# Assembling sixteen rows of x ahead of time, and fetching one channel from SBUF

## The chip, the cores and the metric

The kernel runs on one core of a Trainium2 chip. The metric is the device time of one execution in microseconds (us); the median of three runs of the kernel before the change is 3288.08 us (3287.99 to 3289.75). Lower is better. A core has five engines that follow their own instruction streams in order: TensorE (PE in the profile; its weight loads are PEld), VectorE (DVE), ScalarE (ACT), GpSimd (POOL) and SyncE (SP, which here only starts transfers). Transfers are moved by 16 DMA engines; the kernel starts them from SP, a few from ACT, and those that add to their destination from POOL. All data are 32-bit floats.

## The reference, cut to what matters

The input x is a 384 x 384 grid of vectors of 128 channels. Two layers follow each other.

Layer 0 normalises each vector over its channels to z, forms `left` and `right`, each a matrix product of z times a sigmoid gate of z, and multiplies them channel by channel:

```python
core = jnp.einsum('bikh,bjkh->bijh', left, right)
zo = _layernorm(core, onorm_g, onorm_b) @ Wout + bout
g = jax.nn.sigmoid(x @ Wg + bg)
return x + g * zo
```

So for each of 128 channels `core` is a 384 x 384 x 384 matrix product, and the following layer norm goes over the channels: its statistics are complete only when the last channel is.

Layer 1 works on each row of the result: `left * right_sum * gate`, where `right_sum` is a sum over the row, then a product with `W_out`, the residual, and a layer norm over the channels.

## The kernel before, in words

There are three stages. The order on each engine is the order of the program's text, since every instruction goes through `seq`, which keeps it.

**Stage 1** (0 to about 1131 us of the profile) walks over x in chunks, normalises, transposes (line 279), makes `left` and `right` (lines 331 to 342) and writes them channel by channel to DRAM as `lr_d`. On the way it stores two other things in DRAM: the transposed rows of `x - nd`, where `nd` is one number per vector made from its mean and deviation, as `xt_d` (line 302), and these numbers as `nd_d` (line 310). Thus x, transposed, is `nd_d` broadcast to all partitions plus `xt_d`.

**Stage 2** (about 1131 to 1875 us) is a loop over the 128 channels h. For each h there are nine matmuls of 128x384 (line 501), each of which the profile shows as two instructions, with `t` (left) and `rr` (right) as operands. `load_h` (lines 86 to 95) loads channel h+3 when h is done with its buffer; `fill(h + 1)` on POOL copies the right part out of the interleaved load (lines 476 to 483); ACT copies the product out of PSUM (line 510) and squares it (511), DVE adds both to the running sums `csum` and `csq` (512, 513), and SP stores the channel to `core_d` (517). The last channel, h = 127, is handled apart (lines 518 to 536): block 0 of its product, rows 0 to 127 of the output, is computed first and stored in two parts (first 16 rows, then 112), then DVE finishes the variance of those rows, ACT takes the square root, and DVE's `inverse` and `newton` give the reciprocal standard deviation `r` (lines 427 to 449). POOL then sends `r` to DRAM as `rstd_d` (line 533) and squares and adds the other two blocks (lines 534 to 536).

**Stage 3** (about 1875 us to the end) is a software pipeline over the 384 rows. Iteration t contains, in this order: `front`, which transposes rows of x if needed and makes the layer-0 gate; the loads that are due; `scale_core(t)`, core times `r` (`cs`); `layer0(t - 2)`, the output product `pr` of layer 0 (line 674) and two DVE instructions that give `x1T`; `gated_left(t - 3)`, two matmuls of layer 1 (691, 692); and for rows whose group's sum is known, `layer1`, the statistics and the norms. Rows 0 to 3 take `r` not from DRAM but through a matmul with a column of the identity (`pb`, line 662), and their `cs` is made by DVE (663); from row 4 on POOL makes it (665) with `rt`, read from `rstd_d`. No `cs` can be made before all 128 channels of the row's `ct` have arrived.

For rows below TR = 16, x comes from the input itself: four rows at a time are loaded (line 570), each row is transposed by three PE instructions (line 640) and copied out of PSUM by ACT or DVE (642, 644). From row 16 on, `load_x` broadcasts `nd_d` into SBUF (576) and `add_x` lets POOL start a transfer that adds `xt_d` to it (584); no transpose is needed. `front` runs ahead of the rows: A = 9 rows at t = 0, and at least L = 4 rows for x, with the gate L rows behind.

At the start of stage 3 SP's order is: x of rows 0 to 11 (three loads), core of rows 0 to 3 in two parts (channels 0 to 111, then 112 to 127), x of rows 12 to 15, then core and `rt` of rows 4 to 7.

Of the kernel before, what the change touches and what calls it, by code (L numbers as in the profile page):

```python
# [8 lines left out]
F32 = mybir.dt.float32  # L9
AF = mybir.ActivationFunctionType  # L10
ALU = mybir.AluOpType
# [3 lines left out]
P = 128  # L15
# [4 lines left out]
def triangle_then_gated_row_kernel(ctx: ExitStack, tc: tile.TileContext, a: dict, out: bass.AP):  # L20
# [9 lines left out]

    nc = tc.nc
    x = a["x"].rearrange("b i j c -> (b i) j c")
    y = out.rearrange("b i j c -> (b i) j c")
    N, _, C = x.shape
# [6 lines left out]
    KEEP = 2  # L43
    RG = 4
    A = 9
    L = 4
    TR = 16

    cpool = ctx.enter_context(tc.tile_pool(name="const", bufs=1))
# [3 lines left out]
    rstd_d = dpool.tile([N, N], F32, name="rstd_d")  # L53
    xt_d = dpool.tile([C, N, NB, P], F32, name="xt_d")
    nd_d = dpool.tile([N, N], F32, name="nd_d")

    def seq(ins):

        return tc.keep_in_program_order(ins)
# [21 lines left out]
    with ExitStack() as ctx2:  # L81
# [369 lines left out]
        with tc.tile_pool(name="p2r", bufs=2, side="right", reuse_waits="tile") as rrp, \  # L451
# [14 lines left out]
            def fill(h):  # L466

                if h < H:
# [15 lines left out]
                    if h == 0:  # L484
                        stay()

            fill(0)
            for h in range(H):
                fill(h + 1)
                t, rr = loaded2.pop(h), right.pop(h)  # L490
                pc = ps.tile([P, NB, 512], F32, tag="pc", name="pc")
                banks = [pc[:, ib, :N] for ib in range(NB)]
                order = [(kb, ib) for kb in range(NB) for ib in range(NB)]
                if h == H - 1:


                    banks[0] = ps1.tile([P, 512], F32, name="pc0")[:, :N]
                    order.sort(key=lambda o: o[1] > 0)
                    seq(nc.scalar.activation(warm, mhalf[:, 0:1], AF.Sqrt, scale=-1.0))
                for kb, ib in order:  # L500
                    seq(nc.tensor.matmul(  # L501
                        banks[ib], lhsT=t[:, kb, ib * P:(ib + 1) * P, 0], rhs=rr[:, kb],
                        start=(kb == 0), stop=(kb == NB - 1),
                    ))

                ct = op.tile([P, NB, N], F32, tag="ct", name="ct")
                sq = qp.tile([P, NB, N], F32, tag="sq", name="sq")
                to = core_d[:, h, :].rearrange("(b p) j -> p b j", p=P)
                if h < H - 1:
                    seq(nc.scalar.copy(ct, pc[:, :, :N]))  # L510
                    seq(nc.scalar.activation(sq, ct, AF.Square))
                    seq(nc.vector.tensor_add(csum, csum, ct))  # L512
                    seq(nc.vector.tensor_add(csq, csq, sq))
                    load_h(h + 3)

                    queue = nc.sync if h < H - 3 else nc.scalar
                    seq(queue.dma_start(out=to, in_=ct))
                else:
                    seq(nc.scalar.copy(ct[:, 0], banks[0]))
                    seq(nc.scalar.activation(sq[:, 0], ct[:, 0], AF.Square))  # L520
                    seq(nc.scalar.dma_start(out=to[:16, 0], in_=ct[:16, 0]))
                    seq(nc.scalar.dma_start(out=to[16:, 0], in_=ct[16:, 0]))
                    seq(nc.vector.tensor_add(csum[:, 0], csum[:, 0], ct[:, 0]))
                    seq(nc.vector.tensor_add(csq[:, 0], csq[:, 0], sq[:, 0]))
                    seq(nc.scalar.copy(ct[:, 1:], pc[:, 1:, :N]))
                    variance(0, slice(0, N))
                    root(0)
                    inverse(0, slice(0, N))
                    newton(0, slice(0, N))
                    seq(nc.scalar.dma_start(out=to[:, 1:], in_=ct[:, 1:]))  # L530


                    seq(nc.gpsimd.dma_start(out=rstd_d[0:P, :], in_=roots[0][1]))
                    seq(nc.gpsimd.tensor_tensor(sq[:, 1:], ct[:, 1:], ct[:, 1:], ALU.mult))
                    seq(nc.gpsimd.tensor_tensor(csum[:, 1:], csum[:, 1:], ct[:, 1:], ALU.add))
                    seq(nc.gpsimd.tensor_tensor(csq[:, 1:], csq[:, 1:], sq[:, 1:], ALU.add))
# [5 lines left out]
    with ExitStack() as ctx3:  # L542
        def pool(name, bufs, **kw):
            return ctx3.enter_context(tc.tile_pool(name=name, bufs=bufs, reuse_waits="tile", **kw))


        xp, lp, fp, inp = pool("p3x", 6), pool("p3l", 20), pool("p3f", A), pool("p3in", 3)
        wp, sp, op, up = pool("p3w", 4), pool("p3s", 4), pool("p3out", 3), pool("p3u", 18)
        ps2, ps = pool("p3ps2", 4, space=PSUM), pool("p3ps", 4, space=PSUM)

        def bank(name):
            return ps.tile([P, 512], F32, tag="bank", name=name)

        def work(name, pool=wp):
            return pool.tile([P, N], F32, tag=name, name=name)

        def work_x(name):

            return lp.tile([P, N], F32, tag="x", name=name)

        cols = [slice(b * P, (b + 1) * P) for b in range(NB)]
        lnsb = lns.unsqueeze(1).to_broadcast([P, NB, C])
# [2 lines left out]

        def load_x(i0):

            if i0 < TR:
                xt = xin[i0] = xp.tile([P, RG, N], F32, tag="xt", name="xn")
                seq(nc.sync.dma_start(  # L570
                    out=xt.rearrange("p i (b c) -> p i b c", b=NB),
                    in_=x[i0:i0 + RG].rearrange("i (b p) c -> p i b c", p=P),
                ))
            elif i0 < N:
                xt = xts[i0] = xp.tile([P, RG, N], F32, tag="xt", name="xt")
                seq(nc.sync.dma_start(
                    out=xt.rearrange("p i j -> p (i j)"),
                    in_=nd_d[i0:i0 + RG].rearrange("i j -> (i j)").partition_broadcast(P),
                ))

        def add_x(i0):
# [4 lines left out]
                    in_=xt_d[:, i0:i0 + RG].rearrange("c i b k -> c (i b k)"), accum_op=ALU.add,  # L586
                ))

        def load_core(i0):
            if i0 < N:  # L590
                ct = inp.tile([P, RG, N], F32, tag="ct", name="ct")

                for hs in (slice(0, H),) if i0 > 0 else (slice(0, H - 16), slice(H - 16, H)):
                    seq(nc.sync.dma_start(out=ct[hs], in_=core_d[i0:i0 + RG, hs].rearrange("i h j -> h i j")))
                rt = None
                if i0 > 0:
                    rt = inp.tile([P, RG, N], F32, tag="rt", name="rt")
                    seq(nc.sync.dma_start(
                        out=rt.rearrange("p i j -> p (i j)"),
                        in_=rstd_d[i0:i0 + RG].rearrange("i j -> (i j)").partition_broadcast(P),  # L600
                    ))
                cin[i0] = ct, rt
# [20 lines left out]

        def front(f):

            r = rows.get(f - L)
            if r:
                pg = bank("pg")
                seq(nc.tensor.matmul(pg[:, :N], lhsT=wg0, rhs=r["xT"], start=True, stop=True))  # L629
                gT = r["gT"] = work("gT", fp)  # L630
                seq(nc.scalar.activation(gT, pg[:, :N], AF.Sigmoid, bias=bg0))  # L631
            if f < N:
                i0, n = f // RG * RG, f % RG
                if f >= TR:
                    xT = xts[i0][:, n]
                else:
                    xT = work_x("xT")
                    pxt = ps2.tile([P, 512], F32, tag="py", name="pxt") if f < A else bank("pxt")
                    for s in cols:
                        seq(nc.tensor.transpose(pxt[:, s], xin[i0][:, n, s], ident))  # L640
                    if 4 <= f < A:
                        seq(nc.vector.tensor_copy(xT, pxt[:, :N]))
                    else:
                        seq(nc.scalar.copy(xT, pxt[:, :N]))
                rows[f] = {"xT": xT}

        def right_sums(i0, i1):

# [18 lines left out]
        def layer0(i):  # L667

            r = rows[i]
            m, n = group[i]  # L670
            if n == 0:
                quad[m] = {"tot": sp.tile([P, 16], F32, tag="tot", name="tot")}
            pr = bank("pr")
            seq(nc.tensor.matmul(pr[:, :N], lhsT=wc, rhs=r["cs"], start=True, stop=True))  # L674
            seq(nc.vector.scalar_tensor_tensor(pr[:, :N], pr[:, :N], bz, r["gT"], ALU.add, ALU.mult))
            x1T = r["x1T"] = work_x("x1T")
            seq(nc.vector.scalar_tensor_tensor(
                x1T, pr[:, :N], bout1, r["xT"], ALU.add, ALU.add, accum_out=quad[m]["tot"][:, n:n + 1]
            ))
# [104 lines left out]
                ))  # L784
            stores.clear()

        for i0 in range(0, 3 * RG, RG):
            load_x(i0)
        load_core(0)
        load_x(3 * RG)  # L790
        load_core(RG)

        pieces = [(variance, b, s) for b in range(1, NB) for s in cols]
        pieces += [(root, b, None) for b in range(1, NB)]
# [1 line left out]
        f, fetched, added = 0, TR, TR  # L796
        for t in range(N + 3):

            while f < min(N + L, t + max(L, A - t // 3)):
                front(f)  # L800
                f += 1
            if t % RG == 0:
                load_core(t + 2 * RG)
            if t >= 2 and fetched <= f + 16:
                load_x(fetched)
                fetched += RG
            if t >= 9 and t % 4 == 1:
# [88 lines left out]
```

## Time and profile before

| | |
|---|---|
| median of three runs | 3288.08 us |
| the profiled execution's own time | 3288.67 us |
| its span, first to last instruction | 3286.9 us |
| PE busy | 3266.7 us, 99% of the span |
| DVE, ACT, POOL busy | 2489.0, 1933.7, 2280.3 us |
| PE transposes of x in stage 3 (line 640) | 48 instructions |
| bytes moved | 873.71 MB, 266 GB/s over the span |

"Busy" is the time in which an engine had an instruction in work; on PE instructions overlap, so that the duration of one is longer than the step from one to the next. A line such as L501 is that line of the kernel. "Idle before, releaser" says what ended an engine's wait. The span lies 1.8 us below the profiled execution's own time, and that time is 0.6 us above the median.

### The profile page before, as it was taken

The page shows a single profiled execution, that of the slowest core. Times are in us where ns is not written, and L with a number is a line of the kernel's source. Part 1 is how long each engine was busy: PE and PEld are TensorE (multiplying, and loading weights), DVE is VectorE, ACT ScalarE, POOL GpSimd, SP SyncE. Part 2 cuts the span into 40 slices and gives each one's busy share as a digit, 9 for nine tenths or more (in the row PEclk, how much of TensorE's full clock was granted, in tenths as well). Part 3 has the DMA queues.
Part 4 walks back from the last instruction along what each step waited for, and adds up shares of the span by engine and source line. Part 5 has one row for each costly group of instructions (what it writes and reads, how often), then busy time and mean ns, then how long its engine had stood idle before and what let it go on. Part 6 is the DMA issues. An engine that isn't in the chain of part 4 may idle for free.

```text
span 3286.9 us, 48330 instructions
## 1 busy us (share of the span) xinstructions
PE 3266.7 (99%) x12460; PEld 1989.3 (61%) x12460; DVE 2489.0 (76%) x8022; ACT 1933.7 (59%) x4056; POOL 2280.3 (69%) x3301
## 2 busy tenths in 40 slices
PE   9999999999999999999999999999999999999998
PEld 4544444444444566666666666667777777777776
DVE  7777777777777655555555688888888888888888
ACT  4555555555555533333333467677777777777776
POOL 6555555555555555556666578888888888888997
PEclk9999999999999999999999999999999999999999
DMA  6998998999999499999999999999999999999994
GB/s 164 274 278 259 276 282 259 276 280 265 271 279 271 147 280 282 285 284 282 282 282 283 285 294 266 279 276 272 273 280 277 269 278 276 272 272 274 268 253 128
DMA packets 922055, 873.71 MB, mean 266 GB/s; under 512 B 24834, under 2 KB 836868, under 8 KB 921780
## 3 DMA queue, kind: packets, MB, share of 16 engines
q1 hardware_dynamic: 906532, 796.03, 78.5%
q0 software_dynamic: 13440, 72.56, 12.8%
q8 instruction: 102, 1.67, 0.2%
q10 hardware_dynamic: 1808, 2.03, 0.2%
q14 instruction: 173, 1.42, 0.1%
HBM read 508.63 MB, written 361.89 MB: 265 GB/s over the span
## 4 chain that ended last, share of the span: by engine, by line
PE 92%; POOL 5%; ACT 1%; issue 1%; DVE 1%; DMA 0%; POOLq 0%; ACTq 0%; DVEq 0%
PE pr L331 30%; PE pc L501 22%; PE py L703 7%; PE pg L629 6%; PE pl L692 6%; PE pr L674 6%; PE pg L691 6%; PE pt L279 4%; PE py L704 3%; POOL rs L723 1%; POOL yt L773 1%; POOL cs L665 1%; ACT py L738 1%; POOL nm L726 0%; POOL rs L722 0%
## 5 line engine op out<-in xcount | busy, mean ns | idle before, releaser
L331 PE MATMUL pr<-wz,zt 128*128 128x512 f32 x2304 | 1039.9, 593 | 0.0
L340 ACT ACTIVATE sg<-pr,rs 128x256 f32<-128x256 f32 x1152 | 482.9, 470 | 497.7 <-PE pr L331 363.8
L501 PE MATMUL pc<-rr,lrh 128*128 128x384 f32 x2304 | 743.3, 486 | 0.3 <-DVE lr L342 0.3
L342 DVE SCALAR_TENSOR_TENSOR lr<-pr,rs,sg 128x256 f32<-128x256 f32 x1152 | 504.6, 480 | 267.4 <-ACT sg L340 219.0
L331 PEld LDWEIGHTS pr<-wz,zt 128*128 128x128 f32 x2304 | 414.6, 191 | 410.7 <-issue 345.2
L501 PEld LDWEIGHTS pc<-rr,lrh 128*128 128x128 f32 x2304 | 452.4, 196 | 291.4 <-issue 1.1
L738 ACT ACTIVATE py<-py,nm,rs 128x128 f32<-128x128 f32 x1149 | 493.0, 430 | 197.8 <-POOL rs L727 116.8
L703 PEld LDWEIGHTS py<-wo,u 128*128 128x128 f32 x2304 | 376.8, 191 | 97.4
L512 DVE TENSOR_TENSOR csum<-csum,ct 128x1152 f32<-128x1152 f32 x127 | 179.1, 1410 | 337.9 <-ACT ct L510 337.9
L665 POOL TENSOR_TENSOR cs<-ct,rt 128x384 f32<-128x384 f32 x380 | 426.0, 1125 | 10.7 <-DMA rt<-rstd_d 5.4
L773 POOL TENSOR_TENSOR yt<-yt,lnb 128x384 f32<-128x384 f32 x380 | 423.8, 1117 | 3.1 <-DVE yt L767 3.1
L510 ACT COPY ct<-pc 128x1152 f32<-128x1152 f32 x127 | 142.1, 1119 | 445.3 <-PE pc L501 441.6
L703 PE MATMUL py<-wo,u 128*128 128x128 f32 x2304 | 402.1, 275 | 0.0
L260 POOL TENSOR_SCALAR sd<-mv 128x8 f32<-128x8 f32 (+1 forms) x145 | 28.5, 197 | 427.4 <-DVE mv L247 427.3
L270 POOL TENSOR_TENSOR z<-xt,nd 128x512 f32<-128x512 f32 x287 | 298.7, 1041 | 36.1 <-POOL z L270 30.9
L718 DVE BATCH_NORM_STATS2 st<-py 128x6 f32<-128x128 f32 x1152 | 265.6, 286 | 68.5 <-PE py L704 66.5
L704 PE MATMUL py<-ident,x1T 128*128 128x128 f32 x1152 | 314.1, 273 | 0.0
L674 PE MATMUL pr<-cs,wc 128*128 128x384 f32 x768 | 313.9, 491 | 0.0
L692 PE MATMUL pl<-x1T,mat_L_conv_W_left 128*128 128x384 f32 x768 | 311.0, 487 | 0.9 <-ACT gT L631 0.8
L691 PE MATMUL pg<-x1T,mat_L_conv_W_gate 128*128 128x384 f32 x768 | 310.8, 487 | 1.0 <-ACT g L694 0.9
L629 PE MATMUL pg<-xt,mat_L_conv_Wg 128*128 128x384 f32 x736 | 298.9, 488 | 1.3 <-ACT gT L631 1.3
L482 POOL COPY rr<-lrh 128x768 f32<-128x768 f32 x128 | 182.7, 1427 | 160.7 <-DMA lrh<-lr_d 160.2
(134 smaller groups left out, 4898.1 us busy)
## 6 DMA issues: line engine op xcount, KB each, us to landing
lr_d<-lr SPq DMA_DIRECT2D x128, 1024.0 KB, 7.2
lrh<-lr_d SPq DMA_DIRECT2D x128, 768.0 KB, 7.8
xt_d<-zt SPq DMA_DIRECT2D x288, 256.0 KB, 5.4
xt<-in_x_dram SPq DMA_DIRECT2D x143, 512.0 KB, 6.5
ct<-core_d SPq DMA_DIRECT2D x95, 768.0 KB, 6.2
rt<-rstd_d SPq DMA_DIRECT2D x95, 768.0 KB, 7.7
out_dram<-yt SPq DMA_DIRECT2D x94, 768.0 KB, 8.8
core_d<-ct SPq DMA_DIRECT2D x125, 576.0 KB, 8.8
```

The source lines that it names most:

```text
L331: seq(nc.tensor.matmul(pr[:, r, :], lhsT=zts[n, q][:, 2 * half + r, :], rhs=wz, start=True, stop=True))
L340: seq(nc.scalar.activation(sg[r], pr[:, r, 2 * H:], AF.Sigmoid, scale=rs[r]))
L342: seq(nc.vector.scalar_tensor_tensor(t[:, :, c * XR + r0 + r, :], pr[:, r, :2 * H].rearrange("k (h s) -> k h s", s=2), rs[r], sg[r].rearra ...
L501: seq(nc.tensor.matmul(banks[ib], lhsT=t[:, kb, ib * P:(ib + 1) * P, 0], rhs=rr[:, kb], start=(kb == 0), stop=(kb == NB - 1),))
L629: seq(nc.tensor.matmul(pg[:, :N], lhsT=wg0, rhs=r["xT"], start=True, stop=True))
L665: seq(nc.gpsimd.tensor_tensor(cs, ct[:, i % RG], rt[:, i % RG], ALU.mult))
L674: seq(nc.tensor.matmul(pr[:, :N], lhsT=wc, rhs=r["cs"], start=True, stop=True))
L691: seq(nc.tensor.matmul(pg2[:, :N], lhsT=wgate, rhs=r["x1T"], start=True, stop=True))
L692: seq(nc.tensor.matmul(pl[:, :N], lhsT=wleft, rhs=r["x1T"], start=True, stop=True))
L703: seq(nc.tensor.matmul(py[:, s], lhsT=r["u"][:, s], rhs=r["wo"], start=True, stop=False))
L738: seq(nc.scalar.activation(py[:, s], py[:, s], AF.Identity, bias=bias, scale=scale))
L773: seq(engine.tensor_tensor(yt, yt, lnbb, ALU.add))
```

## The change

Four things are changed.

1. In stage 2, `early_x(h)` puts together the transposed x of rows 0 to 15, one row in every five channels: SP broadcasts a row of `nd_d` into a buffer (h = 6 + 5i), POOL starts a transfer that adds `xt_d` (h = 8 + 5i), and SP stores the result to a new DRAM tensor `xf_d` (h = 11 + 5i).
2. Stage 3 loads the first 16 rows from `xf_d`, four rows at a time, already transposed. The transposes, their copies out of PSUM and the distance L are gone; `front` is the gate alone, one row ahead at least and nine at t = 0. Nine gates use eight PSUM buffers of both pools.
3. Block 0 of the last channel is copied to a tile of its own, `last_h`, and stored to `core_d` in one transfer. For rows 0 to 3 the last channel no longer comes through `core_d`: four transfers on POOL's queue copy one row each from `last_h` into partition 127 of `ct`. SP's second part now holds channels 111 to 126 (16 partitions).
4. SP's order at the start of stage 3 becomes: x of rows 0 to 7, core channels 0 to 111, x of rows 8 to 11, core channels 111 to 126, core and `rt` of rows 4 to 7, x of rows 12 to 15. Loads of later rows of x are called by the row in work (t + 18) and no longer by the row of `front`. Buffers: `x1T` 18 of its own, `gT` 12 (were 9), `u` 17 (were 18).

```diff
+            def early_x(h):
+                for n, step in enumerate((6, 8, 11)):
+                    i, odd = divmod(h - step, 5)
+                    if not odd and 0 <= i < TR:
+                        if n == 0:
+                            early[i] = rp.tile([P, N], F32, tag="ve", name="xe", bufs=NB)
+                            seq(nc.sync.dma_start(out=early[i], in_=nd_d[i].partition_broadcast(P)))
+                        elif n == 1:
+                            seq(nc.gpsimd.dma_start(
+                                out=early[i], in_=xt_d[:, i].rearrange("c b k -> c (b k)"), accum_op=ALU.add
+                            ))
+                        else:
+                            seq(nc.sync.dma_start(out=xf_d[:, i], in_=early.pop(i)))
...
+            last_h = rp.tile([P, N], F32, tag="r", name="last_h", bufs=NB)
             fill(0)
             for h in range(H):
                 fill(h + 1)
+                early_x(h)
...
-                    seq(nc.scalar.copy(ct[:, 0], banks[0]))
-                    seq(nc.scalar.activation(sq[:, 0], ct[:, 0], AF.Square))
-                    seq(nc.scalar.dma_start(out=to[:16, 0], in_=ct[:16, 0]))
-                    seq(nc.scalar.dma_start(out=to[16:, 0], in_=ct[16:, 0]))
+                    seq(nc.scalar.copy(last_h, banks[0]))
+                    seq(nc.scalar.activation(sq[:, 0], last_h, AF.Square))
+                    seq(nc.scalar.dma_start(out=to[:, 0], in_=last_h))
...
-        xp, lp, fp, inp = pool("p3x", 6), pool("p3l", 20), pool("p3f", A), pool("p3in", 3)
-        wp, sp, op, up = pool("p3w", 4), pool("p3s", 4), pool("p3out", 3), pool("p3u", 18)
+        xp, lp, fp, inp = pool("p3x", 6), pool("p3l", 18), pool("p3f", A + 3), pool("p3in", 3)
+        wp, sp, op, up = pool("p3w", 4), pool("p3s", 4), pool("p3out", 3), pool("p3u", 17)
...
-                for hs in (slice(0, H),) if i0 > 0 else (slice(0, H - 16), slice(H - 16, H)):
+                for hs in (slice(0, H),) if i0 > 0 else (slice(0, H - 16), slice(H - 17, H - 1)):
                     seq(nc.sync.dma_start(out=ct[hs], in_=core_d[i0:i0 + RG, hs].rearrange("i h j -> h i j")))
+                    if i0 == 0 and hs.start == 0:
+                        for i in range(RG):
+                            seq(nc.gpsimd.dma_start(out=ct[H - 1:H, i], in_=last_h[i:i + 1]))
+                    if between and hs.start == 0:
+                        between()
...
-            r = rows.get(f - L)
-            if r:
-                pg = bank("pg")
-                seq(nc.tensor.matmul(pg[:, :N], lhsT=wg0, rhs=r["xT"], start=True, stop=True))
-                gT = r["gT"] = work("gT", fp)
-                seq(nc.scalar.activation(gT, pg[:, :N], AF.Sigmoid, bias=bg0))
-            if f < N:
-                i0, n = f // RG * RG, f % RG
-                if f >= TR:
-                    xT = xts[i0][:, n]
-                else:
-                    xT = work_x("xT")
-                    pxt = ps2.tile([P, 512], F32, tag="py", name="pxt") if f < A else bank("pxt")
-                    for s in cols:
-                        seq(nc.tensor.transpose(pxt[:, s], xin[i0][:, n, s], ident))
-                    if 4 <= f < A:
-                        seq(nc.vector.tensor_copy(xT, pxt[:, :N]))
-                    else:
-                        seq(nc.scalar.copy(xT, pxt[:, :N]))
-                rows[f] = {"xT": xT}
+            r = rows[f] = {"xT": xts[f // RG * RG][:, f % RG]}
+            pg = ps2.tile([P, 512], F32, tag="py", name="pg") if f < A and f % 2 == 0 else bank("pg")
+            seq(nc.tensor.matmul(pg[:, :N], lhsT=wg0, rhs=r["xT"], start=True, stop=True))
+            gT = r["gT"] = work("gT", fp)
+            seq(nc.scalar.activation(gT, pg[:, :N], AF.Sigmoid, bias=bg0))
...
-        for i0 in range(0, 3 * RG, RG):
-            load_x(i0)
-        load_core(0)
+        load_x(0)
+        load_x(RG)
+        load_core(0, between=lambda: load_x(2 * RG))
+        load_core(RG)
         load_x(3 * RG)
-        load_core(RG)
...
-            while f < min(N + L, t + max(L, A - t // 3)):
+            while f < min(N, t + max(1, A - t // 2)):
                 front(f)
                 f += 1
             if t % RG == 0:
                 load_core(t + 2 * RG)
-            if t >= 2 and fetched <= f + 16:
+            if t >= 2 and fetched <= t + 18:
```

In the program's order on POOL the four transfers of `last_h` stand behind line 533 (`rstd_d`) and lines 534 to 536, since stage 3's text comes after stage 2's; in `front` nine gates stand ahead of the first `pb`, a tenth behind it, then two more `pb`, and then `pr` of row 0.

More of the change, by code (lines that the diff above doesn't have):

```diff
@@ L45, in triangle_then_gated_row_kernel @@
     A = 9
-    L = 4
     TR = 16
@@ L55, in triangle_then_gated_row_kernel @@
     nd_d = dpool.tile([N, N], F32, name="nd_d")
+    xf_d = dpool.tile([C, TR, N], F32, name="xf_d")
     def seq(ins):
@@ L485, in fill @@
                         stay()
+            def early_x(h):
[11 more added lines that the diff above has]
+                            seq(nc.sync.dma_start(out=xf_d[:, i], in_=early.pop(i)))
+            early = {}
+            last_h = rp.tile([P, N], F32, tag="r", name="last_h", bufs=NB)
             fill(0)
@@ L518, in triangle_then_gated_row_kernel @@
                 else:
-                    seq(nc.scalar.copy(ct[:, 0], banks[0]))
-                    seq(nc.scalar.activation(sq[:, 0], ct[:, 0], AF.Square))
-                    seq(nc.scalar.dma_start(out=to[:16, 0], in_=ct[:16, 0]))
-                    seq(nc.scalar.dma_start(out=to[16:, 0], in_=ct[16:, 0]))
-                    seq(nc.vector.tensor_add(csum[:, 0], csum[:, 0], ct[:, 0]))
+                    seq(nc.scalar.copy(last_h, banks[0]))
+                    seq(nc.scalar.activation(sq[:, 0], last_h, AF.Square))
+                    seq(nc.scalar.dma_start(out=to[:, 0], in_=last_h))
+                    seq(nc.vector.tensor_add(csum[:, 0], csum[:, 0], last_h))
                     seq(nc.vector.tensor_add(csq[:, 0], csq[:, 0], sq[:, 0]))
@@ L555, in work @@
             return pool.tile([P, N], F32, tag=name, name=name)
-        def work_x(name):
-            return lp.tile([P, N], F32, tag="x", name=name)
         cols = [slice(b * P, (b + 1) * P) for b in range(NB)]
@@ L566, in load_x @@
         def load_x(i0):
[L568 to L574, printed above, removed]
+            if i0 < N:
                 xt = xts[i0] = xp.tile([P, RG, N], F32, tag="xt", name="xt")
@@ L577, in load_x @@
                     out=xt.rearrange("p i j -> p (i j)"),
-                    in_=nd_d[i0:i0 + RG].rearrange("i j -> (i j)").partition_broadcast(P),
+                    in_=xf_d[:, i0:i0 + RG].rearrange("c i j -> c (i j)") if i0 < TR
+                    else nd_d[i0:i0 + RG].rearrange("i j -> (i j)").partition_broadcast(P),
                 ))
@@ L587, in add_x, with load_core @@
                 ))
-        def load_core(i0):
+        def load_core(i0, between=None):
             if i0 < N:
                 ct = inp.tile([P, RG, N], F32, tag="ct", name="ct")
-                for hs in (slice(0, H),) if i0 > 0 else (slice(0, H - 16), slice(H - 16, H)):
+                for hs in (slice(0, H),) if i0 > 0 else (slice(0, H - 16), slice(H - 17, H - 1)):
                     seq(nc.sync.dma_start(out=ct[hs], in_=core_d[i0:i0 + RG, hs].rearrange("i h j -> h i j")))
+                    if i0 == 0 and hs.start == 0:
[3 more added lines that the diff above has]
+                        between()
                 rt = None
@@ L675, in layer0 @@
             seq(nc.vector.scalar_tensor_tensor(pr[:, :N], pr[:, :N], bz, r["gT"], ALU.add, ALU.mult))
-            x1T = r["x1T"] = work_x("x1T")
+            x1T = r["x1T"] = work("x1T", lp)
             seq(nc.vector.scalar_tensor_tensor(
```

## The prediction

> **What bounds the kernel now.** I read the page first, then PE's waits and busy time by stage, then the timeline around the start of stage 3. The page's engine line:
>
> ```profile
> PE 3266.7 (99%) x12460; PEld 1989.3 (61%) x12460; DVE 2489.0 (76%) x8022; ACT 1933.7 (59%) x4056; POOL 2280.3 (69%) x3301
> ```
>
> PE has 20 us of idle time in all, so a gain must be PE work removed, and any wait put into PE's stream is paid in full. Busy time by stage (PE, PEld, DVE, ACT, POOL, then clock, DMA share, GB/s):
>
> ```profile
> 1131.00:1874.80 743.80, 743.48 (x2308) 452.78 (x2307) 404.20 (x262) 293.13 (x261) 446.33 (x764) 1.00 0.92 282
> 1874.80:1920.00 45.20, 44.16 (x186) 28.25 (x185) 34.21 (x82) 23.61 (x47) 18.95 (x20) 1.00 0.98 335
> 2000.00:3250.00 1250.00, 1247.18 (x5968) 878.75 (x5967) 1095.62 (x3865) 912.58 (x2099) 1095.55 (x1496) 1.00 0.96 268
> 3275.00:3280.00 5.00, 0.00 (x0) 0.00 (x0) 4.48 (x12) 3.71 (x9) 4.10 (x8) 0.70 0.31 88
> 3280.00:3287.00 7.00, 0.00 (x0) 0.00 (x0) 0.81 (x2) 0.00 (x0) 0.43 (x1) 0.50 0.39 108
> ```
>
> Stage 2 leaves PE 0.3 us of idle time, the 45 us at the start of stage 3 leave 1.04, the body 2.8 in 1250. DMA is at 0.92 in stage 2. The last two rows: PE does its last work at 3273.2, and a mean clock of 0.70 in 3275:3280 means that it fell to 0.50 at 3277.0.
>
> PE's waits from 1850 to 1960, all three:
>
> ```profile
> PE pxt L640 <- ACT ct L525: 0.6, 1, 0.6
> PE pg L629 <- ACT xT L644: 0.2, 1, 0.2
> PE pg L691 <- DVE x1T L677: 0.2, 1, 0.2
> ```
>
> The timeline at the seam, a later transposed row, and GpSimd's four small transfers at the kernel's start:
>
> ```profile
> 1.04 3.78 PE L156 MATMUL p<-avg 128*128 128x512 f32 x4 [1.04 <-DVE mhalf L140]
> ...
> 1.47 0.76 POOL L65 DMA_DIRECT2D stage<-in_L_conv_bl_dram  x1 [0.18 <-issue]
> 2.23 0.51 POOL L65 DMA_DIRECT2D stage<-in_L_conv_br_dram  x1
> ...
> 1880.13 0.56 DVE L449 SCALAR_TENSOR_TENSOR r<-r,m 128x384 f32<-128x384 f32 x1
> 1880.99 0.67 POOL L533 DMA_DIRECT2D rstd_d<-r  x1 [13.07 <-DVE r L449]
> 1881.68 1.48 POOL L534 TENSOR_TENSOR sq<-ct 128x768 f32<-128x768 f32 x1
> 1883.11 1.82 POOL L535 TENSOR_TENSOR csum<-csum,ct 128x768 f32<-128x768 f32 x1
> 1884.88 1.81 POOL L536 TENSOR_TENSOR csq<-csq,sq 128x768 f32<-128x768 f32 x1
> 1886.24 0.81 PE L674 MATMUL pr<-cs,wc 128*128 128x384 f32 x2
> ...
> 1898.30 0.49 PE L640 MATMUL pxt<-ident,xn 128*128 128x128 f32 x3
> 1898.63 0.81 PE L674 MATMUL pr<-cs,wc 128*128 128x384 f32 x2
> 1899.28 0.81 PE L691 MATMUL pg<-x1T,mat_L_conv_W_gate 128*128 128x384 f32 x2
> ```
>
> POOL waits 13 us for `r`, which is ready at 1880.69, then works until 1886.69. The first `pr` runs at 1886.24. A row's three transposes take 0.33 us of PE (1898.30 to 1898.63), a 128x384 product 0.65.
>
> [...] half clock 3.8 us after PE's last work[...]. [...] GpSimd's four 0.5 KB transfers at the start land 3.3, 3.7, 4.2 and 4.0 us after issue, the 192 KB of `rstd_d` after 6.6. [...]
>
> **Removed.** 48 transposes: 16 rows x 0.325 = 5.2 us of PE. Their copies on ACT and DVE (0.4 to 0.5 us each) cost nothing before, except for the first two waits. Of the 1.04 us of PE idle time at the seam, 0.4 stays: the second gate needs a PSUM buffer that ACT's L525 frees at 1875.58, and the first gate ends at 1875.23.
>
> **Added: the wait for the last channel.** `cs` of row 0 needs partition 127 of `ct`. Its transfer now stands on POOL behind L533, which waits for `r`, and behind three additions. So it cannot start before 1886.7, though `last_h` is ready at 1873.2. Issue of the first 0.76 us, of each next 0.5; landing as the 0.5 KB transfers, 3.3 us after issue: 1890.0. DVE's product 0.55, semaphore 0.1: `pr` of row 0 can start at 1890.7. What has PE until then? From 1874.58 one gate (to 1875.23), from 1875.63 eight more at 0.65 (to 1880.83), `pb` (`r` just came), a gate, two `pb`: 4 x 0.65, to 1883.4. ACT's sigmoids (2.05 us for four) start at 1877.7 and free the buffers in time. Then PE stands at the first `pr`, everything else queued behind it: 7.3 us. Rows 1 to 3 land by about 1890.8, 1891.7 and 1892.5, one step ahead of PE's use or a few tenths behind it (DVE makes three `cs` before the first `x1T`: 0 to 0.4 us).
>
> Bounds: [...] if it takes `rstd_d`'s 6.6, 10.6. [...]
>
> **Clock.** [...] so the clock halves before 1890.7. [...] I take 2.3, and no x1T wait beside it, since a slow PE hides that.
>
> **Other seam work.** SP's second core part overlaps channel 111, so it waits for the first part to land (10.8 us from about 1871), then 3.6: under 1886, covered by the wait for `last_h`. x of rows 8 to 11 comes behind the first part, needed at 1880: same cover. `rt` of rows 4 to 7 waits for `rstd_d` as before (1887.6). POOL's four issues (2.3 us) lie before its first `cs`, which waits to 1892.1 for `rt` anyway.
>
> **Stage 2.** Per five channels: a broadcast (192 KB), an adding transfer and a store. The trace's packets of 1536 bytes take 65 ns: 128 x 65 / 16 = 0.52 us each for broadcast and store. Adding packets of 6144 bytes take 573 ns (276 for plain ones); a quarter is 143 ns, so 1.15. Sum 2.2 us, against an idle share of 0.08 x 5.81 = 0.46 us per channel, 2.3 in five: just enough. The largest lump delays the next load by 1.15 - 0.46 = 0.7 us. Cover:
>
> ```profile
> 1505.80 1.99 POOL L482 COPY rr<-lrh 128x768 f32<-128x768 f32 x1 [1.84 <-DMA lrh<-lr_d]
> ...
> 1511.46 0.88 POOL L482 COPY rr<-lrh 128x768 f32<-128x768 f32 x1 [1.70 <-DMA lrh<-lr_d]
> ```
>
> The copy waits for the load to 1505.80, and PE needs it at 1509.05: with 0.9 to 2.0 us of copying (slow only beside DVE's L513, which a later start avoids) 1.3 to 2.4 us are spare. So 0; I take 0.3. If the adding packets cost twice that, 1.15 us per five channels are lacking, and 16 rows could cost up to 18. POOL's issue (0.93) fits into its waits (1.84 for the load, 0.83 for PE), and SP's into 4.2 us of waiting per channel; the store waits for an adding transfer issued 13 us earlier (9.5 to land).
>
> **Elsewhere.** From row 16 on PE's order per row is unchanged; a buffer of `x1T` or `u` is freed by the row finished one iteration earlier. 0.
>
> Sum: -5.2 - 0.6 + 7.3 + 2.3 + 0.3 = +4.1 us on the profiled execution's 3288.67 (span 3286.9 + 1.8), and the same on the median: 3292.2.
>
> **Rivals.** (B) The wait without most of the clock loss, or a quicker landing: about 3289.9. [...] Chance 0.18. (C) Stage 2's queue fills up: 0.5 us per row lost, 8 us, 3300; it decides when the adding packet costs over some 160 ns. For it the share of 0.92; against it the spare 1.3 to 2.4 us. 0.13. (D) `last_h` lands as late as `rstd_d`: +3.3, 3295.5; for it SP's loads that start at 1887.6 and share the engines; 0.15. (E) The transfers land before they are needed, so that only -5.8 remains: 3282.3; against it POOL's order; 0.04. The forecast has 0.50.
>
> **How the numbers follow.** 0.2% (6.6 us) is about what a measurement of this kernel can tell from no change: 3281.5 to 3294.7. Faster: a part of E, 0.02. Slower: C, D and a tenth of the forecast, 0.32. The range 3288.5 to 3299.5 leaves out E, a little of B and the upper part of C.
>
> **What would show it.** Right: POOL's four issues after 1886.7, DVE's first `cs` waiting on them for 7 us, PE idle about 7 us before the first `pr`, clock 0.5 for some 4 us after; stage 2 still 743.8 us long, DMA share near 1.0 in its first two thirds. Wrong: waits of PE on the `rr` copies in stage 2 (C), no wait at the first `pr` (E), or waits in the body of stage 3 that I put at nothing.

## The result and the profile after

The changed kernel takes 3297.62 us (median of nine runs, 3296.18 to 3301.71), the kernel before 3288.08 in the same comparison (nine runs, 3286.57 to 3291.01). The ratio is 1.0030, with a 95% interval of 1.0021 to 1.0038: 9.5 us slower, and even the lower end of the interval lies above the 0.2% that the prediction takes for what can be told from no change. The time lies inside the range of the prediction, 5.4 us above the one it names. Slower by over 0.2% was not its likeliest outcome: it gave that a chance of 0.32.

The profiled execution of the changed kernel is the longest of its nine: 3301.71 us, span 3299.9, which is 13.0 more than the one of before. So a sum made on the two profiles comes out 3.5 us larger than the medians differ.

The page's engine line of the changed kernel, busy us with share and instructions:

```profile
PE 3267.2 (99%) x12412; PEld 1985.1 (60%) x12412; DVE 2488.3 (75%) x8017; ACT 1930.9 (59%) x4045; POOL 2301.8 (70%) x3321
```

The 48 transposes are gone from the count (12460 to 12412), and yet PE is busy for 0.5 us longer. With 13.0 us more span, both facts ask the same question: where was PE slow, and where did it stand?

Busy time by stage in the changed kernel (PE, PEld, DVE, ACT, POOL, then clock, DMA share, GB/s):

```profile
1131.00:1877.00 746.00, 745.21 (x2309) 452.57 (x2308) 409.18 (x265) 294.43 (x264) 462.34 (x780) 1.00 0.94 295
1877.00:1925.00 48.00, 37.81 (x109) 21.57 (x110) 26.00 (x56) 16.17 (x31) 17.35 (x18) 0.86 0.86 289
2005.00:3260.00 1255.00, 1250.68 (x5971) 879.41 (x5971) 1097.89 (x3872) 916.38 (x2106) 1103.00 (x1506) 1.00 0.94 269
```

In stage 2 DMA moves 295 GB/s instead of 282, and PE does not notice: from its first `pc` to its last it needs 742.80 us in both profiles (1132.60 to 1875.40 after, 1131.46 to 1874.26 before). The body stays as tight as it was. The 48 us at the start of stage 3 are the place: PE stands for 10.2 of them, and its mean clock is 0.86.

PE's waits from 1870 to 1960, the first three by size:

```profile
PE pr L678 <- DVE cs L667: 9.2, 1, 9.2
PE pb L666 <- ACT gT L649: 0.7, 1, 0.7
PE pg L647 <- ACT ct L545: 0.6, 1, 0.6
```

The first `pr` waits for 9.2 us, where before it did not wait at all. The timeline of that stretch shows for what:

```profile
1882.14 0.59 POOL L553 DMA_DIRECT2D rstd_d<-r  x1 [13.08 <-DVE r L450]
1882.74 1.49 POOL L554 TENSOR_TENSOR sq<-ct 128x768 f32<-128x768 f32 x1
1884.17 1.81 POOL L555 TENSOR_TENSOR csum<-csum,ct 128x768 f32<-128x768 f32 x1
1885.93 1.80 POOL L556 TENSOR_TENSOR csq<-csq,sq 128x768 f32<-128x768 f32 x1
...
1887.67 2.01 POOL L610 DMA_DIRECT2D ct<-last_h  x4
...
1893.64 1.48 DVE L667 TENSOR_TENSOR cs<-ct,pb 128x384 f32<-128x384 f32 x3 [11.80 <-DMA ct<-last_h]
...
1894.34 1.62 PE L678 MATMUL pr<-cs,wc 128*128 128x384 f32 x2 [9.23 <-DVE cs L667]
```

Read downwards, it is the chain of the prediction: POOL waits 13 us for `r`, sends `rstd_d`, multiplies and adds, and only then issues the four transfers of `last_h`, a tile that ACT had written at 1874.4. DVE's three `cs` wait for the landing, PE for the first `cs`. What differs is the last link. The profile's line on the landing of these four transfers:

```profile
DMA to landing us min/median/max: 5.4/5.5/5.8
```

They take 5.5 us and not 3.3; the first, for which PE waits, takes 5.8. Then the clock, in the same columns as the stages above:

```profile
1888.00:1891.00 3.00, 0.00 (x0) 0.00 (x0) 0.00 (x0) 0.00 (x0) 1.68 (x4) 0.84 1.00 320
1891.00:1895.00 4.00, 0.66 (x1) 0.50 (x2) 1.36 (x3) 0.00 (x0) 0.00 (x0) 0.50 1.02 368
1895.00:1899.00 4.00, 3.33 (x6) 1.45 (x5) 1.37 (x4) 0.58 (x1) 0.99 (x1) 0.50 1.01 419
1899.00:1902.00 3.00, 3.00 (x6) 1.49 (x6) 1.65 (x3) 0.00 (x0) 1.00 (x1) 0.50 0.56 149
1902.00:1904.00 2.00, 2.00 (x5) 1.11 (x4) 0.57 (x3) 0.58 (x1) 0.00 (x0) 0.57 0.92 342
```

The mean of 0.84 in 1888:1891 means a fall near 1890.0, and the 0.57 in 1902:1904 a return near 1903.7; the trace's own clock records have them at 1890.06 and 1903.71. PE works again from 1894.34, so it runs for 9.4 us at half clock, 8.7 of them busy. A 128x384 product takes it 1.28 us there (`pr` at 1899.35, the next product at 1900.63) and 0.64 once the clock is back (1906.04, 1906.68). So half of the 8.7 is lost, an estimated 4.4 us.

At the other end of the kernel, 1.5 us appear that no engine's busy time shows. After GpSimd's last computation the trace's records have a DRAIN, an instruction that stands at the end of its program. It takes 6.71 us before and 8.23 after, and it ends 0.8 us before the span does in both.

### The profile page after: what moved, and what is told of

Same layout as the page of the kernel before. It is cut to its first block, busy times and chain, and to the rows that moved or that the text cites. A ratio compares the mean times of both kernels' runs of the same rounds, so it can differ in the third digit from the quotient of the medians.

```text
span 3299.9 us, 48314 instructions
## 1 busy us (share of the span) xinstructions
PE 3267.2 (99%) x12412; PEld 1985.1 (60%) x12412; DVE 2488.3 (75%) x8017; ACT 1930.9 (59%) x4045; POOL 2301.8 (70%) x3321
## 4 chain that ended last, share of the span: by engine, by line
PE 91%; POOL 5%; DVE 1%; ACT 1%; issue 1%; DMA 1%; POOLq 0%; DVEq 0%; ACTq 0%
PE pr L332 30%; PE pc L522 22%; PE py L707 6%; PE pr L678 6%; PE pl L696 6%; PE pg L695 6%; PE pg L647 6%; PE pt L280 4%; PE py L708 3%; POOL rs L727 1%; POOL cs L669 1%; POOL yt L777 1%; ACT py L742 1%; DMA core_d<-ct 0%; DVE st L722 0%
## 5 line engine op out<-in xcount | busy, mean ns | idle before, releaser
L533 DVE TENSOR_TENSOR csum<-csum,ct 128x1152 f32<-128x1152 f32 x127 | 180.8, 1423 | 334.5 <-ACT ct L531 334.5
L647 PE MATMUL pg<-xt,mat_L_conv_Wg 128*128 128x384 f32 x768 | 311.2, 488 | 2.5 <-ACT gT L649 1.9
L483 POOL COPY rr<-lrh 128x768 f32<-128x768 f32 x128 | 173.5, 1356 | 151.8 <-DMA lrh<-lr_d 151.6
```

## The experiments

In the expectations, W is my theory: the loss is the wait for `last_h`, made by where its transfers stand on GpSimd's queue, together with the half clock that the wait brings. R is the rival: a part of the loss that counts lies elsewhere in the change, in stage 2's added traffic, in stage 3's new loads and buffers, or at the end. Each kernel stands beside runs of before on the same chip: 3288.83 us (median of 55 runs) for e1, e3, e4 and e6, 3289.45 (46 runs) for e5, e7, e8 and e9, 3290.21 (one run) for e10 and e11. Ratios and differences are against these. The 95% intervals of the ratios are 4 to 6 us wide, so differences of 1 or 2 us are read from the traces and not from the medians.

So that the start of a run, which shifts by up to 3 us between executions (the first `pc` of stage 2 starts at 1129.53 in e6_core_d and at 1132.60 in the changed kernel), doesn't count, this table gives PE's position relative to its last `pc` of stage 2, as a difference from the kernel before (start of `pr` of the row, us, from one trace each; after and before included):

| kernel | row 0 | row 3 | row 16 | row 40 | row 383 | GpSimd's DRAIN |
|---|---|---|---|---|---|---|
| before | 0 | 0 | 0 | 0 | 0 | 6.71 |
| after | +7.0 | +11.1 | +9.2 | +10.7 | +10.4 | 8.23 |
| e1_sp | -2.5 | -3.4 | -5.0 | -4.4 | -5.2 | 8.02 |
| e6_core_d | -2.6 | -3.6 | -5.5 | -4.9 | -5.5 | 8.02 |
| e3_fill | +7.1 | +6.3 | +4.5 | +5.8 | +4.6 | 8.22 |
| e4_early | 0.0 | 0.0 | 0.0 | +0.2 | +0.2 | 8.02 |
| e5_pool_order | 0.0 | -1.0 | -2.9 | -1.6 | -2.6 | 8.22 |
| e7_part3 | +6.2 | +7.6 | +7.6 | +8.4 | +8.0 | 6.91 |
| e8_dve_add | -2.7 | -3.8 | -4.2 | -3.8 | -4.4 | 6.71 |
| e9_small | 0.0 | 0.0 | 0.0 | +1.1 | +3.0 | 4.72 |
| e10_small16 | 0.0 | 0.0 | 0.0 | +1.0 | +1.0 | 7.45 |
| e11_small32 | 0.0 | 0.0 | 0.0 | +1.0 | +2.1 | 3.25 |

### e1_sp: the four transfers on SP's queue

```diff
                     seq(nc.sync.dma_start(out=ct[hs], in_=core_d[i0:i0 + RG, hs].rearrange("i h j -> h i j")))
-                    if i0 == 0 and hs.start == 0:
-                        for i in range(RG):
-                            seq(nc.gpsimd.dma_start(out=ct[H - 1:H, i], in_=last_h[i:i + 1]))
                     if between and hs.start == 0:
                         between()
+                    if i0 == 0 and hs.start == 0:
+                        for i in range(RG):
+                            seq(nc.sync.dma_start(out=ct[H - 1:H, i], in_=last_h[i:i + 1]))
```

> The changed kernel, but the four last_h transfers go through SP's queue, behind the load of x rows 8 to 11, where SP waits anyway. Theory W (the loss is the wait for last_h behind GpSimd's work, and the slow clock after it): both are gone; PE reaches the first pr at about 1885 without a wait of more than 1 us, the clock stays at 1.0, the median is 3282 to 3284, 4 to 6 us below the kernel before. Rival R (part of the loss comes from stage 2's extra transfers or from the changed loads and buffers in stage 3): the median stays at 3287 or above.

Measured: 3286.65 us (13 runs), ratio 0.9995 (0.9987 to 1.0003). The wait at the first `pr` is gone, the clock stays at 1.0, and the transfers start at 1875.2 instead of 1887.7 and land sooner. The profile's line on them:

```profile
DMA to landing us min/median/max: 2.3/3.0/4.6
```

PE gets through the last row 5.2 us earlier than before, about the whole price of the 48 transposes. So the queue on which four small transfers stand makes the difference between +9.5 and a kernel that can't be told from before. The median lies above the 3282 to 3284 that W expected and just below R's 3287: of the 5.2 it keeps 2.2. GpSimd's DRAIN takes back 1.3, a part that W did not have and that lies, as R says, elsewhere in the change; the rest lies within what single executions scatter by (3284.15 to 3290.27). The landing took 3.0 us in the median on SP's queue against 5.5 on GpSimd's; the queue is not the only thing that differs, since SP also started 12 us earlier, in other traffic.

### e6_core_d: the last channel through DRAM as before

The other three parts of the change stay; only the route of the last channel of rows 0 to 3 goes back to `core_d`.

```diff
-                for hs in (slice(0, H),) if i0 > 0 else (slice(0, H - 16), slice(H - 17, H - 1)):
+                for hs in (slice(0, H),) if i0 > 0 else (slice(0, H - 16), slice(H - 16, H)):
                     seq(nc.sync.dma_start(out=ct[hs], in_=core_d[i0:i0 + RG, hs].rearrange("i h j -> h i j")))
-                    if i0 == 0 and hs.start == 0:
-                        for i in range(RG):
-                            seq(nc.gpsimd.dma_start(out=ct[H - 1:H, i], in_=last_h[i:i + 1]))
```

> The changed kernel with one part undone: the last channel of rows 0 to 3 comes through core_d again (channels 112 to 127 in SP's second part, no last_h transfers). Theory W: 3282 to 3285, with up to 2 us of wait at the first pr, as the second part waits for the store of the last channel (landing near 1881) and takes 3.6 us. Rival R: 3287 or above.

Measured: 3285.11 us (21 runs), ratio 0.9988 (0.9981 to 0.9994), 3.7 us faster than before. The last row is reached 5.5 us earlier. PE's one wait of note at the seam is 0.3 us for a PSUM buffer, where W had allowed up to 2 us at the first `pr`. So without the short cut from SBUF to SBUF nothing has to wait: the copy through DRAM, which the short cut was to replace, is not late at all.

### e3_fill: the wait stays, PE is kept busy in it

Twelve products of 128x384 that nobody reads are put ahead of the first `pr`, into a buffer of their own; they add work and leave nothing out.

```diff
+            if t == 2:
+                pd = ps2.tile([P, 512], F32, tag="py", name="pd")
+                for _ in range(12):
+                    seq(nc.tensor.matmul(pd[:, :N], lhsT=ident, rhs=xts[0][:, 0], start=True, stop=True))
```

> The changed kernel with 12 matmuls of 128x384 added ahead of the first pr, whose result nobody reads. They fill 7.8 us of PE's 9.2 us wait and so keep the array's clock up, but don't end the wait. Theory W with the clock as a separate part of 4 to 5 us: 3292 to 3294, clock 1.0 throughout. If the clock's share is what was forecast (2.3): 3295. If the clock costs nothing by itself: 3297 to 3298.

Measured: 3294.39 us (19 runs), ratio 1.0017 (1.0011 to 1.0024). The clock stays at 1.00 through the seam, and this is what is left of the wait:

```profile
PE pr L678 <- DVE cs L667: 1.9, 1, 1.9
```

12 x 0.65 + 1.9 = 9.7 us pass before the first `pr`, half a microsecond more than the 9.2 of the changed kernel. The loss is +5.6 instead of +9.5 us, a difference of 4.0 between medians, each of them uncertain by 2 to 3 us: alone it could not tell 4 from the forecast 2.3, and 3294.39 lies between what the two would give. The traces can tell. Both kernels start `pr` of row 0 at the same place (+7.0 and +7.1 in the table). From there to row 16 the changed kernel takes 49.13 us and this one 44.25, with the same work in between. Of these 4.9 us, 0.7 is the wait at a `pb`, which is gone here, and some 4.2 is the half clock itself, near the 4.4 worked out above.

### e4_early: stage 2's part alone

The kernel before with `early_x` and `xf_d` added and `xf_d` not read; stage 3 still transposes its own rows.

```diff
...
+            early = {}
+
             fill(0)
             for h in range(H):
                 fill(h + 1)
+                early_x(h)
```

> The kernel before with early_x added in stage 2 (16 rows put together and stored to xf_d, which nobody reads); stage 3 as before. Theory W: stage 2's extra transfers are hidden: 3288 within 1.5 us, steps of PE from channel to channel at 5.805 us. Rival R: 3291 or above, with PE waiting on rr.

Measured: 3289.75 us (13 runs), ratio 1.0003 (0.9994 to 1.0011). No row of stage 3 starts more than 0.5 us later than before. The added transfers are hidden on PE, and rival C of the prediction falls. The 1.3 us of the longer DRAIN appear at the end of the trace; W, which expected 3288 within 1.5 us, did not have them, and the median can't show them apart from no change.

### e5_pool_order: the same queue, another order on it

The four transfers stay on POOL, and the store of `rstd_d`, with its wait for `r`, is moved behind them.

```diff
-                    seq(nc.gpsimd.dma_start(out=rstd_d[0:P, :], in_=roots[0][1]))
                     seq(nc.gpsimd.tensor_tensor(sq[:, 1:], ct[:, 1:], ct[:, 1:], ALU.mult))
...
                         for i in range(RG):
                             seq(nc.gpsimd.dma_start(out=ct[H - 1:H, i], in_=last_h[i:i + 1]))
+                        seq(nc.gpsimd.dma_start(out=rstd_d[0:P, :], in_=roots[0][1]))
```

> The changed kernel with GpSimd's order alone altered: the three additions come first and no longer behind the wait for r, then the four last_h transfers, then rstd_d. Theory W (it is the place on GpSimd, not the kind of queue): the additions run from about 1877 to 1882, the first last_h transfer starts near 1882.2 and lands 3.3 to 5.9 us later, PE waits 1 to 4 us at the first pr in place of 9.2, the clock stays at 1.0: median 3286 to 3289, 9 to 11 us below the changed kernel. Rival Q (transfers from GpSimd are slow by themselves, wherever they stand): above 3292.

Measured: 3287.45 us (13 runs), ratio 0.9995 (0.9987 to 1.0003). POOL's timeline at the seam:

```profile
1875.10 1.46 POOL L553 TENSOR_TENSOR sq<-ct 128x768 f32<-128x768 f32 x1 [7.74 <-ACT ct L545]
...
1880.05 2.01 POOL L609 DMA_DIRECT2D ct<-last_h  x4
1882.05 0.57 POOL L610 DMA_DIRECT2D rstd_d<-r  x1
```

The additions start as soon as ACT's copy is there, 7.6 us earlier than in the changed kernel (1.7 of it because stage 2 ends earlier in this execution), and so do the transfers, which take 4.1 to 4.8 us from issue to landing. Two waits stay on PE, 1.4 us for `r` at the first `pb` and 1.0 at the first `pr`, and the clock stays full: PE gets from row 0 to row 16 in 2.9 us less than before, as in e6_core_d. So GpSimd's queue as such is not the cause: the place behind the wait for `r` is.

### e7_part3: the short cut alone

The kernel before with part 3 only: `last_h`, its store, and four transfers on POOL behind L533 to L536. The transposes stay.

```diff
...
-                for hs in (slice(0, H),) if i0 > 0 else (slice(0, H - 16), slice(H - 16, H)):
+                for hs in (slice(0, H),) if i0 > 0 else (slice(0, H - 16), slice(H - 17, H - 1)):
                     seq(nc.sync.dma_start(out=ct[hs], in_=core_d[i0:i0 + RG, hs].rearrange("i h j -> h i j")))
+                    if i0 == 0 and hs.start == 0:
+                        for i in range(RG):
+                            seq(nc.gpsimd.dma_start(out=ct[H - 1:H, i], in_=last_h[i:i + 1]))
```

> The kernel before with the last channel of rows 0 to 3 taken from last_h by GpSimd's queue, and nothing else changed (transposes, gates and loads as before). Theory W: PE waits 6 to 7.5 us at the first pr and runs at half clock after it: 3297 to 3301. Rival (the earlier gates of the change made the wait cost more): below 3294.

Measured: 3298.56 us (9 runs), ratio 1.0026 (1.0017 to 1.0036). That is +9.1 us, as much as the whole change costs. The largest of PE's waits at the seam:

```profile
PE pr L677 <- DVE cs L666: 5.4, 1, 5.4
```

The transfers start at 1888.04, as late as in the changed kernel, and land in 4.8 to 5.3 us. PE waits 3.8 us less than in the changed kernel (and less than the 6 to 7.5 that W expected). Counted from the end of stage 2, it gets to this wait 3.0 us later, and the wait ends 0.8 us earlier. It gets there later since eleven of the sixteen rows are still transposed ahead of the first `pr`, 11 x 0.325 = 3.6 us, while three gates fewer stand there than in the changed kernel, 1.9 us; longer waits for buffers and copies make up the rest. The clock, in the columns used above:

```profile
1888.00:1891.00 3.00, 0.43 (x2) 0.00 (x0) 0.00 (x0) 0.00 (x0) 2.01 (x5) 0.94 1.07 405
1891.00:1894.00 3.00, 0.14 (x1) 0.17 (x2) 0.84 (x2) 0.00 (x0) 0.00 (x0) 0.50 1.04 375
1894.00:1897.00 3.00, 3.00 (x5) 1.68 (x6) 2.09 (x6) 0.00 (x0) 0.99 (x1) 0.50 1.03 422
1897.00:1899.00 2.00, 2.00 (x7) 1.14 (x6) 1.47 (x3) 0.51 (x1) 1.00 (x1) 0.89 1.05 422
```

PE works at half clock for 3.6 us here, where it does so for 9.4 in the changed kernel. This says why the change as a whole is no better than its worst part: what it takes away in front of the wait only lengthens the wait, whose end doesn't depend on it, and what it takes away behind the wait (about 2.9 us, by which e6_core_d gets from row 0 to row 16 faster than before) is lost again to the longer half clock, an estimated 2.6 us, and to the wait of 0.7 us at `pb`.

### e8_dve_add: a version that beats both

As e6_core_d, with the addition of `early_x` on VectorE: SP loads `nd_d` and `xt_d` into two tiles, VectorE adds, SP stores.

```diff
                             seq(nc.sync.dma_start(out=early[i], in_=nd_d[i].partition_broadcast(P)))
+                            added[i] = rp.tile([P, N], F32, tag="m", name="xm", bufs=2)
+                            seq(nc.sync.dma_start(out=added[i], in_=xt_d[:, i].rearrange("c b k -> c (b k)")))
                         elif n == 1:
-                            seq(nc.gpsimd.dma_start(
-                                out=early[i], in_=xt_d[:, i].rearrange("c b k -> c (b k)"), accum_op=ALU.add
-                            ))
+                            seq(nc.vector.tensor_add(early[i], early[i], added.pop(i)))
...
```

> As the run in which the last channel comes through core_d again, but the 16 additions of early_x are made by VectorE: SP loads nd_d and xt_d into two buffers, VectorE adds (about 0.5 us, 16 times), SP stores. 16 fewer transfers are started by GpSimd. If GpSimd's DRAIN at the kernel's end (6.71 us with 97 transfers before, 8.02 with 113) counts the transfers that it started: DRAIN back at 6.7, median 1.3 us below that run, 3283 to 3284.5. If DRAIN doesn't count them: 3285, as that run.

Measured: 3283.83 us (21 runs), ratio 0.9984 (0.9978 to 0.9991), 5.6 us faster than before, where the changed kernel is 9.5 slower. GpSimd starts as many transfers as before, and its DRAIN is back at 6.71 us. In this one trace PE loses 1.3 us at a `pr` that waits for POOL's `cs`, and row 383 comes 1.0 later than in e6_core_d, which takes back most of the shorter DRAIN. The intervals of the two kernels overlap as well: that the addition's move alone is a gain is not shown.

### e9_small, e10_small16, e11_small32: what sets the DRAIN

The longer DRAIN went with more transfers started by GpSimd, so a count was the first guess. These kernels are the one before plus 64, 16 or 32 transfers of 512 bytes from GpSimd in stage 2, into a DRAM tensor that nobody reads.

```diff
...
             for h in range(H):
                 fill(h + 1)
+                if h % 2 == 0:
+                    seq(nc.gpsimd.dma_start(out=idle_d[h // 2:h // 2 + 1], in_=ident[0:1, :]))
```

(`h % 8` and `h // 8` for 16, `h % 4` and `h // 4` for 32.)

> The kernel before with 64 more transfers of 512 bytes from GpSimd in stage 2, one in every second channel, to a scratch tensor that nobody reads. If each costs 0.05 us in GpSimd's last DRAIN, as the four small ones of the changed kernel seem to: DRAIN 6.71 + 3.3 = 10.0 us, and the time 3.3 us longer; at 0.08 each: 11.9. If DRAIN is a matter of bytes: 6.7.

> The kernel before with 16 more transfers of 512 bytes from GpSimd in stage 2 (64 of them brought GpSimd's last DRAIN from 6.71 down to 4.72 us). If each transfer adds about 0.05 us and something sets the count back once it passes some number: 6.71 + 0.8 = 7.5 us. If small transfers lower it: about 6.2.

> The same with 32 more transfers. If each adds 0.05 us and nothing has set the count back yet: 8.4 us; if the count was set back by then: below 5. If small transfers lower it: 5.7.

Measured: 3289.63 us (10 runs, ratio 1.0001, 0.9992 to 1.0011) with 64; 3288.46 and 3288.26 in single runs with 16 and 32, beside 3290.21 of before, from which nothing follows for the time. The DRAIN, from the traces' records:

| transfers that GpSimd starts | kernels | DRAIN, us |
|---|---|---|
| 97 | before, e8_dve_add | 6.71 |
| 101 | e7_part3 (4 from SBUF to SBUF) | 6.91 |
| 113 | e1_sp, e4_early, e6_core_d (16 adding ones) | 8.02 |
| 117 | after, e3_fill, e5_pool_order | 8.22 to 8.23 |
| 113 | e10_small16 (16 small ones) | 7.45 |
| 129 | e11_small32 | 3.25 |
| 161 | e9_small | 4.72 |

A plain count falls. The 16 adding transfers lengthen it by 1.30 us, 0.08 each; 16 small ones by 0.74, 0.046 each; and from 129 to 161 small ones it is again 0.046 each (1.47 / 32). Between 113 and 129 it drops: 7.45 + 16 x 0.046 = 8.2 would follow, 3.25 was measured. So it grows with what GpSimd has started and steps back by some 5 us at a point; what is counted, and where it steps back, stays open. The expectation for 64 (10.0, 11.9 or 6.7) was wrong in every branch; of those for 16 and 32 one branch each came true. A shorter DRAIN did not make these kernels faster by as much: with 64 small transfers row 383 comes 3.0 us later, and with 32 it comes 2.1 later, though stage 3 is unchanged, and with 32 the DRAIN ends 1.7 us before the span does. For the change it is enough that the same 1.3 us appear in e4_early, whose only addition is `early_x`, and are gone in e8_dve_add, whose addition isn't GpSimd's.

## Why the prediction was right, and where its sizes were wrong

The mechanism was right, and e1_sp, e5_pool_order, e6_core_d and e7_part3 show it from four sides: moved to another queue, put ahead of the wait for `r`, or taken out, the loss is gone; put alone into the kernel before, it is there in full. The time was 5.4 us too low, from terms of the sum that were too small or missing. That it still lies in the range is owed to the range's width, which left room for D and part of C: two of the nine runs (3300.97 and 3301.71) are above it. The steps:

| step of the sum | predicted | measured |
|---|---|---|
| 48 transposes, waits for PSUM buffers | -5.2, -0.6 | -5.5 together (row 16 of e6_core_d) |
| wait at the first `pr` | +7.3 | +9.2 |
| half clock | +2.3, an estimate | about +4.2 (e3_fill), 4.4 worked out from the trace |
| stage 2 | +0.3 | 0.0 (first to last `pc`), 0.2 in e4_early |
| elsewhere | 0 | +0.7 (`pb`), +1.4 (rows 16 to 40), +1.5 (the end) |

The right column adds up to 11.7 with the trace's terms, near the 11.9 by which the profiled executions differ from the last `pc` on (10.4 to row 383, 1.5 at the end); the medians differ by 9.5, since that execution was the longest of nine.

**Transposes and buffers.** Right in sum to 0.3 us. For the PSUM buffers 0.6 was too much: 0.6 us of that wait stays in the profile after, where I had left 0.4.

**The wait.** POOL's order, the issue right after the additions (1887.67 instead of 1886.7, in an execution whose stage 2 ends 1.15 us later) and 0.5 us for each issue were as forecast. The failing step is "landing as the 0.5 KB transfers, 3.3 us after issue". Those four were taken from the start of the kernel, where the DMA engines are at a share of 0.49 (0 to 5 us); at the seam they are at 0.99 (1887 to 1895), and the first landing took 5.8 us. This made `pr` 2.5 us later, of which PE's own later arrival took back 0.6. The upper bound that I had, `rstd_d`'s 6.6, was the nearer row in place and time, and I put it aside for the nearer size. The medians of the other kernels with these transfers on POOL, 4.6 (e5_pool_order, at a share of 0.66), 5.0 (e7_part3, 1.06) and 5.8 (e3_fill, 0.92), are above 3.3 too. The size alone does not explain it: the 64 transfers of 512 bytes of e9_small, spread over stage 2 at a share of 0.93, land like this:

```profile
DMA to landing us min/median/max: 4.4/4.8/6.1
```

That the traffic makes it is likely; no run varied the traffic alone, and sources and destinations differ as well.

**The clock.** The trace of before has half clock 3.8 us after PE's last work. It doesn't show how long half clock lasts once PE works again, so the 2.3 us and "clock 0.5 for some 4 us after" were my estimate. Measured were 9.4 us of work at half clock. The fall stands at no fixed distance from PE's last work: 4.95 us here (1885.11 to 1890.06), 2.2 in e7_part3. The half clock lasted from 1890.06 to 1903.71, 13.65 us, and in e7_part3 6.83 us, half of that. A quarter of 13.65 is 3.41, and the 1385.81 us from the return to the next fall, at the kernel's end, are 406 times 3.413, so I count in stretches of this length. Counted back from the return, the last three begin at 1893.47, 1896.89 and 1900.30. The first has PE's restart in it at 1894.34. The second holds the 0.67 us in which `pb` waits for a PSUM buffer that ACT frees late (1897.24 to 1897.91), and the clock did not come back after it; it came back after the third, which has no such wait. In e7_part3 the half clock lasts from 1890.61 to 1897.44; PE restarts at 1893.86, the stretch from 1894.02 on has work without a wait, and the clock is back at its end. So in both executions it came back at the end of the first such stretch without a wait. No run varied this wait alone, and that it cost a stretch is not shown beyond these two. I had costed that wait at nothing: "ACT's sigmoids ... free the buffers in time" was right for the gates before the stall, but the eleventh gate, which stands behind the first `pr`, came late with it.

**Stage 2.** Right: 742.80 us as before, in spite of 13 GB/s more. In the slices of the page in which `early_x` runs, DMA moves 299 to 306 GB/s, where 282 was stage 2's mean, and the `pc` of the whole stage take no longer for it.

**Elsewhere.** "0" was wrong in three places. From row 16 to row 40 PE loses 1.4 us more than before, with waits for ACT's `gT` (1.1 us at one `pg`, before 0.5). Some 0.6 of it comes in e1_sp and e6_core_d as well, 1.3 in e3_fill and e5_pool_order, 0.8 in e7_part3. That would fit a part that comes with the transfers of `last_h` on GpSimd; but e9_small, which has none and leaves stage 3 alone, loses 1.1 there too, and e10_small16 and e11_small32 lose 1.0. Its cause stays open. And at the end there is GpSimd's DRAIN, which I didn't look for since no work of the change lies there.

**The rivals.** C (stage 2 fills up) fell with e4_early. E (transfers in time) is false for the change as made and true for e1_sp. D was the right direction: `last_h` lands nearly as late as `rstd_d`'s 6.6 us. D priced this at 3.3 us; the landing itself came to 2.5, and the clock, the late buffer and the DRAIN came on top. The chance of 0.32 for slower by over 0.2% held too little for this: I let the two terms vary one at a time, though the longer wait, the half clock and the late buffer all stand in one stall.

## What to carry to other kernels

A transfer on an engine's queue starts when the engine gets there and not when its data are ready: here the data were ready at 1874.4 and the transfers started at 1887.7. Before putting one on a queue, list the waits that stand ahead of it in the program's order. Time a landing by transfers from the stretch in question, not by one of the same size in a quieter one: 512 bytes on GpSimd's queue took 4.8 us in the median in stage 2, 3.3 to 4.2 at the kernel's start. Where a stall lowers TensorE's clock, count the work behind it as well: in the two executions here, after waits of 5.4 and 9.2 us, 3.6 and 9.4 us of work went by before the clock was back. And work removed ahead of a stall whose end doesn't depend on it only makes the stall longer.

## What the runs showed of the hardware that was not expected

GpSimd's closing DRAIN stands 0.8 us before the end of the span (in e11_small32 1.7) and takes 3.2 to 8.2 us, depending on the transfers that GpSimd started: 0.08 us for each adding transfer of 192 KB, 0.046 for each of 512 bytes, with a drop of about 5 us between 113 and 129 transfers. Sixteen adding transfers that PE doesn't notice where they run still cost 1.3 us there. Small transfers in stage 2 also made the unchanged stage 3 later by 1.0 (16 of them), 2.1 (32) and 3.0 us (64) at row 383, in waits for ACT; one trace each, cause open.

After a stall of 9.2 us TensorE ran at half clock for 9.4 us of work, in which it waited once for 0.67 us; after one of 5.4 us for 3.6 us of work without a wait. Transfers of 1.5 KB from one partition of SBUF to another took 4.1 to 6.0 us from issue to landing on GpSimd's queue (four kernels) and 2.3 to 4.6 on SP's (one kernel).
